# Tighter one-hot windows, table blocks in one go, flushes at their own group's end, and an even pace in a graph kernel

## The chip, the cores and the metric

The kernel runs on one core of one Trainium2 chip. The metric is the device time of one execution in microseconds, as the median of several runs; lower is better. The core has TensorE (PE; its weight loads are listed as PEld), VectorE (DVE), ScalarE (ACT), GpSimd (POOL) and SyncE (SP), which each work through their own instructions in order.

## The reference

12500 nodes have a row x of 128 numbers. 200000 edges have a source node, a destination node and one of four types; the edges come sorted by destination, and the destinations are drawn as 12500 u^2, so low nodes have many edges and high nodes few. What is computed:

```
h   = relu(layernorm(x))                       # 12500 x 128
out = x
for each edge e:  out[dst[e]] += h[src[e]] @ W[type[e]] + b[type[e]]
```

W is 4 x 128 x 128, b is 4 x 128, all in f32.

## The kernel before

**Chunks and the two parts.** The sorted edges are cut into 1563 chunks of 128. The first 480 chunks, those of the nodes with many edges, are the *dense part*: for a node the kernel counts how often each (source, type) occurs, in `count` (line 802: one-hots L814, L818, L819 on VectorE, matmul L823 into pt, ScalarE copies the counts out, L826), and multiplies the counts with the whole table of h in `multiply` (line 847: loads hs from htab, matmuls pa L858, then py L873 and an add to `acc`). The dense part goes over 14 batches of up to 92 nodes; the first has no batch before it whose products could run beside its counts.

**The other 1083 chunks** are taken in 70 groups: 66 of 16 chunks (groups 0 to 65, FULL is 66) and small ones of 12, 8, 4 and 3. `gather` (line 443) fetches a chunk's 128 source rows with one indirect DMA on GpSimd's queue (L449), eight to a buffer `hm`, a half group; there are five such buffers. `sum_up` (line 461) does a group:

1. A one-hot for each chunk on VectorE (L471): its columns are type times window plus the node's offset from the chunk's first node. The *window* is the number of nodes that a chunk can span, a number fixed when the kernel is built (`window_of`, line 111), so a one-hot has K = 4 x window columns.
2. TensorE counts the types per node (L494; L492 in the raw groups), ScalarE copies that (cnt, L498).
3. In four steps of four chunks, TensorE sums the rows by type and node (ps, L509; three bf16 matmuls a chunk, of K columns), and ScalarE copies the sums (sb, L516).
4. TensorE multiplies with b (L524) and, in four f32 matmuls of 16 x window columns, with W (py, L526; the trace has two records of each).
5. VectorE adds each chunk's window of py to `ring` (L538), 16 adds at places that are read from memory. The ring holds 2048 nodes.

**The raw groups.** Groups 0 to 7 (RAW is 8) gather rows of x, and normalise them themselves in f32 (`stats` L382, `normalize` L401, one-hots `ohf`, ps in f32), because the table `htab` of normalised rows isn't there yet. It is made meanwhile: `table` (line 413) is a generator of three steps for a block of rows, two blocks a group: the first normalises on ScalarE and copies a bf16 part (L419), the second subtracts it on VectorE (L421) and copies the next part (L422), the third subtracts again (L424) and sends the block with a DMA on SyncE's queue (L425). Step one runs at the group's start (L1008), steps two and three behind the group's own two halves (`table_steps`, L484). `make_slots` prepares the dense part's slots in the same stage.

**The flushes.** Nodes that no later chunk can touch leave the ring, four blocks of 128 nodes at a time: `put_out` (line 577) and `leave` (line 560) transpose them on TensorE (L568), add x on VectorE (xo, L571), send them by DMA (L573) and clear the ring (memset, L586). `goes` (line 615) says behind which group each flush is due; the first, at group 8, adds 1280 nodes of the ring to `acc` instead. A flush that is due behind a group is put on a list (L1069), and made in the next group, behind its sums and ahead of its py (L521).

**The order.** From group 8 on the dense part is a generator (`dense_work`, line 903) whose steps are issued between the groups' steps: `pace` (line 890) says from the columns of both kinds of work how far the dense part should be after each step. In the first batch a count slot weighs 3.5 times as much as later (`alone_slot`, L907). A scheduler then orders each engine's instructions.

Of the kernel before, what the change touches and what calls it, by code (L numbers as in the profile page):

```python
# [35 lines left out]
F32 = mybir.dt.float32  # L36
BF16 = mybir.dt.bfloat16
# [32 lines left out]
def kernel(  # L70
# [37 lines left out]
    starts_of = [sum(levels[:k]) for k in range(len(levels) + 1)]  # L108
    NS = starts_of[-1]

    def window_of(c):

        c = C0 + (c - C0) // G * G
        a_node = E * ((((c + G) * P / E) ** 2 + 1 / N) ** 0.5 - (c + G) * P / E)
        return next((n for n in range(12, WIN, 4) if (n - 1) * a_node > P + 6 * P**0.5), WIN)

    NDT = -(-ND // P)

# [288 lines left out]
        load_nodes(xt, j0, j1)  # L407
        seen_x[j0] = xt, stats(lambda k: xt[:r, k, :], j1 - j0, r, aheads, "t")


    tabling = []

    def table(j0, j1, r):
        n = j1 - j0
        xt, of = seen_x.pop(j0)
        h = npool.tile([P, XG, D], F32, name="h")
        h3 = npool.tile([P, XG, 3, D], BF16, name="h3")
        normalize(lambda k: xt[:r, k, :], lambda k: h[:r, k, :], n, r, of)
        nc.scalar.copy(h3[:r, :n, 0, :], h[:r, :n, :])  # L419
        yield True  # L420
        nc.vector.tensor_sub(h[:r, :n, :], h[:r, :n, :], h3[:r, :n, 0, :])  # L421
        nc.scalar.copy(h3[:r, :n, 1, :], h[:r, :n, :])  # L422
        yield True
        nc.vector.tensor_sub(h3[:r, :n, 2, :], h[:r, :n, :], h3[:r, :n, 1, :])  # L424
        nc.sync.dma_start(  # L425
            htab.rearrange("(p j) f -> p j f", j=NW)[:, j0:j1, :], h3[:, :n].rearrange("p j c d -> p j (c d)")
        )

    def table_steps():
        for t in list(tabling):  # L430
            if next(t, None) is None:
                tabling.remove(t)

    tables = []
    for j0, j1 in ((0, NL), (NL, NW)):
# [20 lines left out]
        return lambda i, c, n: got[i // HG][:, (i % HG * n + c) * D : (i % HG * n + c + 1) * D]  # L456

    waiting = []
    flushing = []

    def sum_up(t0, g, rows, raw, last):
        win = window_of(C0 + t0)
        K = NT * win
        if raw:
            oh = npool.tile([P, G, P], F32, name="ohf")[:, :, :K]
        else:
            while waiting:
                waiting.pop()()
            oh = opool.tile([P, G, P], BF16, name="oh")[:, :, :K]
        for i in range(g):  # L470
            nc.vector.tensor_scalar(  # L471
                oh[:, i, :], (iota_f if raw else iota_b)[:, :K], keyf[:, t0 + i : t0 + i + 1], None, ALU.is_equal
            )
        if raw:
            for h0 in range(0, g, HG):
                row = lambda k: rows(h0 + k, 0, 1)
                n = min(HG, g - h0)
                of = stats(row, n, P, npool, "")
                normalize(row, row, n, P, of)

                with tc.issue_after(of[2]):
                    while waiting and h0 + HG >= g:
                        waiting.pop()()
                    table_steps()  # L484
        sb = spool.tile([P, G * P], F32, name="sb")[:, : G * K].rearrange("p (g t n) -> p g t n", g=G, t=NT)
        def types():

            ohv = oh.rearrange("p g (t n) -> p g t n", t=NT)
            pc = s_ps.tile([R, G * WIN], F32, name="ps")[:, : G * win].rearrange("p (g n) -> p g n", g=G)
            for t in range(NT):  # L490
                if raw:
                    nc.tensor.matmul(pc[:, :g, :], pick_f[:, t, :], ohv[:, :g, t, :], start=(t == 0), stop=(t == NT - 1))  # L492
                else:
                    nc.tensor.matmul(  # L494
                        pc[t * CG : (t + 1) * CG, :g, :], three, ohv[:, :g, t, :], start=True, stop=True, tile_position=(0, t * CG)
                    )
            cnt = spool.tile([R, G * WIN], BF16, name="cnt")[:, : G * win].rearrange("p (g n) -> p g n", g=G)
            nc.scalar.copy(cnt[:, :g], pc[:, :g])  # L498
            return cnt

        R = N3 if raw else P
        cnt = None if raw else types()
        nparts = 1 if raw else 3
        for i0 in range(0, g, SG):
            i1 = min(i0 + SG, g)
            ps = s_ps.tile([P, SG, P], F32, name="ps")[:, :, :K]
            for i in range(i0, i1):
                for c in range(nparts):
                    mm = nc.tensor.matmul(  # L509
                        ps[:, i - i0, :],  # L510
                        rows(i, c, nparts),
                        oh[:, i, :],
                        start=(c == 0),
                        stop=(c == nparts - 1),
                    )
            nc.scalar.copy(sb[:, i0:i1].rearrange("p g t n -> p g (t n)"), ps[:, : i1 - i0, :])  # L516
            yield i1 / g, mm.ins
        if raw:
            cnt = types()

        while flushing:  # L521
            put_out(*flushing.pop(0))
        py = (x_ps.tile([P, G * WIN], F32, name="pt") if last else y_ps.tile([P, G * WIN], F32, name="py"))[:, : G * win].rearrange("p (g n) -> p g n", g=G)
        nc.tensor.matmul(py[:, :g, :], b12 if raw else b128, cnt[:, :g, :], start=True, stop=False)  # L524
        for t in range(NT):
            mm = nc.tensor.matmul(py[:, :g, :], wsb[:, t, :], sb[:, :g, t, :], start=False, stop=(t == NT - 1))  # L526

        def add_up():
            _, at = nc.values_load_multi_w_load_instructions(
                brow[0:1, t0 : t0 + g],  # L530
                engines=[DVE],
                min_val=0,
                max_val=RING - 1,
                skip_runtime_bounds_check_because="the row is clamped to this range on the chip",
            )
            for i in range(g):
                to = ring[:, bass.ds(at[i], win)]
                nc.vector.tensor_tensor(to, to, py[:, i, :], ALU.add)  # L538

        if raw or t0 + g == TM:  # L540
            waiting.append(add_up)
        else:
            add_up()
        yield 1, mm.ins
# [59 lines left out]

    flushes = [(ja, jb, due(jb)) for ja, jb, _ in flushes]


    ends_in = [12, 8, 4, 3]
    FULL = (TM - sum(ends_in)) // G
    r = TM - sum(ends_in) - FULL * G  # L610
    sizes = [G] * FULL + ([r] if r else []) + ends_in
    starts = [sum(sizes[:i]) for i in range(len(sizes))]
# [289 lines left out]

    def dense_work():


        a_slot = float(NB)
        alone_slot = 3.5 * NB  # L907
        a_node = NW * 3.0 * NT
        total = dense_columns() + sum(len(slots_of(u)) for u in units(batches[0])) * (alone_slot - a_slot)
        gone = 0.0  # L910
        before = None
        for vs in batches + [None]:
            steps = {}
            now = None
            if vs:
                now = vs, dense.tile([P, NW, VB // 2 * NT], U16, name="counts")
                steps[count(*now)] = sum(len(slots_of(u)) for u in units(vs)) * (a_slot if before else alone_slot)
            if before:
                steps[multiply(*before)] = len(before[0]) * a_node
            done = {st: 0.0 for st in steps}  # L920
            while done:
                st = min(done, key=done.get)
                part = next(st, None)
                if part is None:
                    del done[st]
                    gone += steps[st]
                else:
                    done[st] = part
                    yield (gone + sum(done[st] * steps[st] for st in done)) / total
            before = now  # L930
# [19 lines left out]
    for gi, (t0, g) in enumerate(zip(starts, sizes)):  # L950
        raw = gi < RAW
        if gi == 0:
# [44 lines left out]
            for t in range(NT):  # L997
                for c in range(3):
                    k = c * NT + t
                    nc.sync.dma_start(b128[t * CG + c : t * CG + c + 1, :], b12[k : k + 1, :])  # L1000
            tabling += [table(*a) for a in tables[:2]]
            table_steps()
            for a in tables[2:4]:
                look(*a)
            done = 2
        elif raw:
            rows = gather(t0, g, x, D)
            tabling += [table(*a) for a in tables[done : done + 2]]  # L1008
            table_steps()
            for a in tables[done + 2 : done + 4]:  # L1010
                look(*a)
            done += 2
            if gi == 1:
                prep_dense()
            elif gi == 3:
                prep_edges(1, 3, prep, QB)
        else:
            rows = gather(t0, g, htab, D3)

            q = (t0 + 8 * G) // P  # L1020
            if (t0 + 8 * G) % P < G and 3 <= q < BM:
                prep_edges(q, q + 1, later, 1)
        if gi == RAW - 1:
            assert done >= len(tables) and not tabling

        behind = ExitStack()
        if gi >= FULL:
# [38 lines left out]
                leave(ja, jb, acc, ja * P)  # L1066
        for (ja, jb, _), i in zip(flushes, goes):
            if i == gi < final - 1:
                flushing.append((ja, jb, True))  # L1069
        if gi == final:  # L1070

            for ahead in (True, False):
# [137 lines left out]
```

## Time and profile before

| | before |
|---|---|
| median of 3 runs | 1923.1 us (1918.42 to 1924.55) |
| profiled execution | 1924.55 us |
| its span, from the first to the last instruction | 1922.7 us |
| mean granted TensorE clock | 0.878 of full speed |
| instructions | 30094 |
| gathers from htab / from x | 955 / 128 |
| last ring add of group 7, of group 9, of the last group | 318.4, 373.8, 1915.8 us |

The profile is of one execution. The busy time of an engine is given in us and as a share of the span. The chain that ended last is followed back from the last instruction, at each step to what released it. A line such as `ACT sb L516 <- remote: 259.0, 51, 8.9` says that ScalarE, at line 516, waited 259.0 us in all, 51 times, at most 8.9 us; "remote" or "unknown queue" is a releaser that the profile doesn't name. A line of the chain or the timeline begins with its start and its length in us; x12 is twelve instructions in a row. By stage the run falls into the raw groups (0 to some 300 us), the main stage with the dense part beside the groups (to some 1870 us), and the end.

### The profile page before, as it was taken

How to read it: one execution, taken by the hardware profiler on the slowest of the kernel's cores; microseconds unless marked ns; L12 is line 12 of the kernel's file. 1: busy time of each engine (PE TensorE's matmuls, PEld its weight loads, DVE VectorE, ACT ScalarE, POOL GpSimd, SP SyncE). 2: the span in 40 equal slices, each digit the busy share in tenths (PEclk: the TensorE clock that was granted, in tenths of full speed). 3: DMA queues.
4: the chain of work that ended last, by engine and by line, in shares of the span. 5: the costliest groups of instructions: out<-in, count | busy, mean ns of one | idle time of the engine just before them, and what ended most of it. 6: DMA issues, size and time to landing. Idle time of an engine off the chain costs nothing.

```text
span 1922.7 us, 30094 instructions
## 1 busy us (share of the span) xinstructions
PE 1421.5 (74%) x9606; PEld 879.8 (46%) x9606; DVE 968.3 (50%) x5293; ACT 589.9 (31%) x1920; POOL 1048.6 (55%) x1093
## 2 busy tenths in 40 slices
PE   0354665776778778787787888787878888788885
PEld 0232432554445445454454455454545545454553
DVE  3666753755556554354344444454565555555233
ACT  3464633222132232323232322323232332323111
POOL 7463455353555546555455566455565666565561
PEclk9995665787888889899799889888999999998998
DMA  4342223454555445455455555455555555455552
GB/s 137 91 138 77 99 82 97 121 153 115 145 148 144 135 124 167 134 175 161 130 154 157 163 150 174 132 169 155 153 151 169 166 146 175 144 162 139 163 166 72
DMA packets 137427, 270.75 MB, mean 141 GB/s; under 512 B 26316, under 2 KB 73598, under 8 KB 137262
## 3 DMA queue, kind: packets, MB, share of 16 engines
q1 hardware_dynamic: 87326, 166.44, 28.2%
q0 software_dynamic: 49936, 102.34, 19.8%
q8 instruction: 76, 1.25, 0.3%
q14 instruction: 89, 0.73, 0.1%
HBM read 252.64 MB, written 16.03 MB: 140 GB/s over the span
## 4 chain that ended last, share of the span: by engine, by line
PE 55%; another core or an unknown queue 14%; DVE 12%; issue 11%; ACT 5%; POOL 2%; DMA 1%; SPq 0%; DVEq 0%; ACTq 0%; POOLq 0%
PE pa L858 29%; PE pt L823 10%; PE ps L509 6%; PE py L526 6%; ACT counts L826 3%; DVE o L819 2%; POOL hm L449 2%; DVE st L382 1%; DVE ring L538 1%; DVE o L818 1%; DVE oh L471 1%; ACT sb L516 1%; PE py L873 1%; PE ps L492 1%
## 5 line engine op out<-in xcount | busy, mean ns | idle before, releaser
L449 POOL DMA_INDIRECT hm<-htab,srcT x955 | 921.5, 965 | 732.8 <-issue 253.0
L858 PE MATMUL pa<-counts,hs 128*128 128x368 fp8e4 (+1 forms) x4116 | 786.1, 339 | 34.1 <-issue 31.9
L858 PEld LDWEIGHTS <-hs 128*128 128x128 bf16 x4116 | 425.9, 104 | 376.4 <-issue 180.2
L823 PE MATMUL pt<-o,o 128*128 128x392 bf16 x1083 | 307.0, 358 | 178.6 <-ACT counts L826 64.7
L826 ACT ACTIVATE counts<-pt 128x392 uint16<-128x392 f32 x630 | 310.3, 504 | 346.3 <-PE pt L823 146.5
L819 DVE TENSOR_SCALAR o<-iota_n,hkT 128x392 bf16<-128x392 f16 x1083 | 350.6, 324 | 0.6 <-issue 0.4
L516 ACT COPY sb<-ps 128x256 f32<-128x256 f32 (+5 forms) x271 | 111.4, 417 | 538.7 <-remote 259.0
L538 DVE TENSOR_TENSOR ring<-ring,py 128x16 f32 (+4 forms) x1056 | 178.8, 169 | 149.5 <-remote 39.8
L814 DVE TENSOR_SCALAR o<-iota_b,loT 128x128 bf16<-128x128 bf16 x375 | 96.2, 257 | 286.5 <-remote 133.8
L509 PE MATMUL ps<-oh,hm 128*128 128x64 bf16 (+4 forms) x2865 | 174.1, 206 | 72.3 <-issue 67.2
L509 PEld LDWEIGHTS <-hm 128*128 128x128 bf16 x2865 | 143.4, 102 | 135.0 <-issue 107.5
L471 DVE TENSOR_SCALAR oh<-iota_b,keyT 128x64 bf16<-128x64 bf16 (+4 forms) x955 | 166.7, 255 | 65.4 <-remote 22.4
L818 DVE TENSOR_SCALAR o<-iota_b,loT,byT 128x128 bf16<-128x128 bf16 x333 | 108.0, 324 | 176.0 <-remote 73.5
L823 PEld LDWEIGHTS <-o 128*128 128x128 bf16 x1083 | 102.8, 104 | 190.9 <-issue 86.2
L449 POOL DMA_INDIRECT hm<-in_x_dram,srcT x128 | 125.6, 981 | 106.1 <-PE ps L509 67.3
L526 PE MATMUL py<-sb,wsb 128*128 128x384 f32 (+4 forms) x528 | 165.9, 460 | 0.7 <-issue 0.7
L509 PE MATMUL ps<-ohf,hm 128*128 128x48 f32 x256 | 60.1, 397 | 107.8 <-ACT hm L401 107.8
L826 ACT ACTIVATION_READ_ACCUMULATOR counts<-pt 128x1 f32 x630 | 131.9, 209 | 0.0
L526 PEld LDWEIGHTS py<-sb,wsb 128*128 128x128 f32 x528 | 107.3, 214 | 51.8 <-issue 26.4
L498 ACT CAST cnt<-ps 128x256 bf16<-128x256 f32 (+7 forms) x70 | 28.5, 407 | 292.6 <-PE ps L494 80.5
L509 PEld LDWEIGHTS ps<-ohf,hm 128*128 128x128 f32 x256 | 54.1, 305 | 126.2 <-ACT hm L401 112.7
L818 DVE TENSOR_SCALAR o<-iota_b,loT 128x128 bf16<-128x128 bf16 x375 | 97.0, 259 | 16.5 <-PE pt L823 12.7
(188 smaller groups left out, 647.2 us busy)
## 6 DMA issues: line engine op xcount, KB each, us to landing
hs<-htab SPq DMA_DIRECT2D x336, 384.0 KB
hm<-htab,srcT POOLq DMA_INDIRECT x955
htab<-h SPq DMA_DIRECT2D x11, 768.0 KB
xo<-in_x_dram SPq DMA_DIRECT2D x23, 256.0 KB
out_dram<-xo SPq DMA_DIRECT2D x23, 256.0 KB
xt<-in_x_dram SPq DMA_DIRECT2D x6, 512.0 KB
hs<-htab SPq DMA_DIRECT2D x14, 192.0 KB
xt<-in_x_dram SPq DMA_DIRECT2D x5, 448.0 KB
```

Of the source, the lines that this page charges most:

```text
L449: nc.gpsimd.indirect_dma_start(out=rows[:, (i - h0) * width : (i - h0 + 1) * width], out_offset=None, in_=table, in_offset=bass.IndirectOf ...
L471: nc.vector.tensor_scalar(oh[:, i, :], (iota_f if raw else iota_b)[:, :K], keyf[:, t0 + i : t0 + i + 1], None, ALU.is_equal)
L509: mm = nc.tensor.matmul(ps[:, i - i0, :], rows(i, c, nparts), oh[:, i, :], start=(c == 0), stop=(c == nparts - 1),)
L516: nc.scalar.copy(sb[:, i0:i1].rearrange("p g t n -> p g (t n)"), ps[:, : i1 - i0, :])
L526: mm = nc.tensor.matmul(py[:, :g, :], wsb[:, t, :], sb[:, :g, t, :], start=False, stop=(t == NT - 1))
L538: nc.vector.tensor_tensor(to, to, py[:, i, :], ALU.add)
L814: nc.vector.tensor_scalar(o1[:, k, :], iota_b, loT[:, s : s + 1], None, ALU.is_equal)
L818: nc.vector.tensor_scalar(o1[:, k, :], iota_b, loT[:, s : s + 1], by, ALU.is_equal, ALU.mult)
L819: nc.vector.tensor_scalar(o2[:, k, :], iota_n, hkT[:, s : s + 1], None, ALU.is_equal)
L823: nc.tensor.matmul(pb, o1[:, k, :], o2[:, k, :], start=first, stop=last)
L826: nc.scalar.activation(counts[:, :, i * NT : (i + 1) * NT], pb.rearrange("p (b t) -> p b t", t=NT), AF.Copy, accum_out=both[:, i : i + 1],)
L858: nc.tensor.matmul(pa[:, : nv * NT], hs[:, j - j0, c * D : (c + 1) * D], counts[:, j, : nv * NT], start=(j == 0 and c == 0), stop=(j == NW ...
```

## The change

Four things are changed. (1) `window_of` goes in steps of 2 from 8 with five deviations of room, where it went in steps of 4 from 12 with six; the small last groups share one number; the buffers of the one-hots and of sb are as wide as the widest window needs. (2) `table` is no longer a generator: a block is made in one go at the start of its raw group. (3) A flush is made at the end of the group behind which it is due, not in the next group. (4) The first dense batch's count slots weigh as much as those of the others.

```diff
     def window_of(c):
-        c = C0 + (c - C0) // G * G
-        a_node = E * ((((c + G) * P / E) ** 2 + 1 / N) ** 0.5 - (c + G) * P / E)
-        return next((n for n in range(12, WIN, 4) if (n - 1) * a_node > P + 6 * P**0.5), WIN)
+        m = min((c - C0) // G, FULL)
+        end = (C0 + (m + 1) * G if m < FULL else T) * P / E
+        a_node = E * ((end**2 + 1 / N) ** 0.5 - end)
+        return next((n for n in range(8, WIN, 2) if (n - 1) * a_node > P + 5 * P**0.5), WIN)
...
     def table(j0, j1, r):
...
         nc.scalar.copy(h3[:r, :n, 0, :], h[:r, :n, :])
-        yield True
         nc.vector.tensor_sub(h[:r, :n, :], h[:r, :n, :], h3[:r, :n, 0, :])
         nc.scalar.copy(h3[:r, :n, 1, :], h[:r, :n, :])
-        yield True
         nc.vector.tensor_sub(h3[:r, :n, 2, :], h[:r, :n, :], h3[:r, :n, 1, :])
...
-            oh = opool.tile([P, G, P], BF16, name="oh")[:, :, :K]
+            oh = opool.tile([P, G, KM], BF16, name="oh")[:, :, :K]
...
-                with tc.issue_after(of[2]):
-                    while waiting and h0 + HG >= g:
-                        waiting.pop()()
-                    table_steps()
+            with tc.issue_after(of[2]):
+                while waiting:
+                    waiting.pop()()
...
-        while flushing:
-            put_out(*flushing.pop(0))
...
-        alone_slot = 3.5 * NB
...
-        total = dense_columns() + sum(len(slots_of(u)) for u in units(batches[0])) * (alone_slot - a_slot)
+        total = dense_columns()
...
-                steps[count(*now)] = sum(len(slots_of(u)) for u in units(vs)) * (a_slot if before else alone_slot)
+                steps[count(*now)] = sum(len(slots_of(u)) for u in units(vs)) * a_slot
...
-            tabling += [table(*a) for a in tables[done : done + 2]]
-            table_steps()
+            for a in tables[done : done + 2]:
+                table(*a)
...
             if i == gi < final - 1:
-                flushing.append((ja, jb, True))
+                put_out(ja, jb, True)
```

The windows, in nodes, by group:

| groups | before | after |
|---|---|---|
| 0 to 7 | 12 | 10 |
| 8 to 12 | 12 | 12 |
| 13 to 15 | 16 | 12 |
| 16 to 24 | 16 | 14 |
| 25 to 28 | 16 | 16 |
| 29 to 32 | 20 | 16 |
| 33 to 40 | 20 | 18 |
| 41 to 44 | 20 | 20 |
| 45 to 49 | 24 | 20 |
| 50 to 57 | 24 | 22 |
| 58 to 60 | 24 | 24 |
| 61 to 65 | 28 | 24 |
| 66 to 69 (the small ones) | 28 | 26 |

More of the change, by code (lines that the diff above doesn't have):

```diff
@@ L109 @@
     NS = starts_of[-1]
+    ends_in = [12, 8, 4, 3]
+    FULL = (TM - sum(ends_in)) // G
     def window_of(c):
-        c = C0 + (c - C0) // G * G
-        a_node = E * ((((c + G) * P / E) ** 2 + 1 / N) ** 0.5 - (c + G) * P / E)
-        return next((n for n in range(12, WIN, 4) if (n - 1) * a_node > P + 6 * P**0.5), WIN)
+        m = min((c - C0) // G, FULL)
+        end = (C0 + (m + 1) * G if m < FULL else T) * P / E
+        a_node = E * ((end**2 + 1 / N) ** 0.5 - end)
+        return next((n for n in range(8, WIN, 2) if (n - 1) * a_node > P + 5 * P**0.5), WIN)
     NDT = -(-ND // P)
@@ L408, in look @@
         seen_x[j0] = xt, stats(lambda k: xt[:r, k, :], j1 - j0, r, aheads, "t")
-    tabling = []
     def table(j0, j1, r):
@@ L427, in table @@
         )
[L429 to L432, printed above, removed]
     tables = []
@@ L458 @@
     waiting = []
-    flushing = []
+    KR, KM = NT * window_of(C0 + RAW * G - 1), NT * window_of(T - 1)
     def sum_up(t0, g, rows, raw, last):
@@ L464, in sum_up @@
         if raw:
-            oh = npool.tile([P, G, P], F32, name="ohf")[:, :, :K]
+            oh = npool.tile([P, G, KR], F32, name="ohf")[:, :, :K]
         else:
@@ L479, in sum_up @@
                 normalize(row, row, n, P, of)
-                with tc.issue_after(of[2]):
-                    while waiting and h0 + HG >= g:
-                        waiting.pop()()
-                    table_steps()
-        sb = spool.tile([P, G * P], F32, name="sb")[:, : G * K].rearrange("p (g t n) -> p g t n", g=G, t=NT)
+            with tc.issue_after(of[2]):
+                while waiting:
+                    waiting.pop()()
+        sb = spool.tile([P, G * KM], F32, name="sb")[:, : G * K].rearrange("p (g t n) -> p g t n", g=G, t=NT)
         def types():
@@ L605 @@
     flushes = [(ja, jb, due(jb)) for ja, jb, _ in flushes]
-    ends_in = [12, 8, 4, 3]
-    FULL = (TM - sum(ends_in)) // G
     r = TM - sum(ends_in) - FULL * G
@@ L1000 @@
                     nc.sync.dma_start(b128[t * CG + c : t * CG + c + 1, :], b12[k : k + 1, :])
-            tabling += [table(*a) for a in tables[:2]]
-            table_steps()
+            for a in tables[:2]:
+                table(*a)
             for a in tables[2:4]:
@@ L1007 @@
             rows = gather(t0, g, x, D)
-            tabling += [table(*a) for a in tables[done : done + 2]]
-            table_steps()
+            for a in tables[done : done + 2]:
+                table(*a)
             for a in tables[done + 2 : done + 4]:
@@ L1023 @@
         if gi == RAW - 1:
-            assert done >= len(tables) and not tabling
+            assert done >= len(tables)
         behind = ExitStack()
```

## The prediction, made blind

> **What bounds the kernel now.** I read the page's busy times first, then the chain that ended last, then the waits, then the chain and the timeline of one stretch in the middle of the run.
>
> ```profile
> PE 1421.5 (74%) x9606; PEld 879.8 (46%) x9606; DVE 968.3 (50%) x5293; ACT 589.9 (31%) x1920; POOL 1048.6 (55%) x1093
> ...
> PE 55%; another core or an unknown queue 14%; DVE 12%; issue 11%; ACT 5%; POOL 2%; DMA 1%; SPq 0%; DVEq 0%; ACTq 0%; POOLq 0%
> PE pa L858 29%; PE pt L823 10%; PE ps L509 6%; PE py L526 6%; ACT counts L826 3%; DVE o L819 2%; POOL hm L449 2%; DVE st L382 1%; DVE ring L538 1%; DVE o L818 1%; DVE oh L471 1%; ACT sb L516 1%; PE py L873 1%; PE ps L492 1%
> ```
>
> The reader is to see that TensorE is the fullest engine and carries most of the chain, half of that in the dense part (L858, L823), which the change leaves alone. What it makes smaller, ps L509 and py L526, is 6% each. The waits tell who waits for TensorE:
>
> ```profile
> POOL hm L449 <- issue: 289.0, 946, 0.6
> ACT sb L516 <- remote: 259.0, 51, 8.9
> POOL hm L449 <- PE pt L823: 246.2, 54, 19.3
> POOL hm L449 <- PE ps L509: 230.7, 44, 15.2
> ```
>
> GpSimd's gathers stand 477 us (246.2 + 230.7) in 98 waits until TensorE frees a row buffer, so from group 8 on the gathers follow TensorE. But the second line (columns: us in all, times, longest) is a wait of another kind: ScalarE and VectorE stand together for up to 9 us with no releaser that the profile names. In the trace about 116 such joint stalls, one per half group, end within some 0.1 us of the landing of the eighth gather of a batch; the batches start 13.7 us apart on average, and some 60% of them 13 us or less, where eight gathers of 1.25 us with a landing of about 2 us leave little to shorten. TensorE starves in these stalls:
>
> ```profile
> 1010.25 0.18 DVE L538 TENSOR_TENSOR ring<-ring,py 128x20 f32 x1
> 1010.49 0.17 DVE L538 TENSOR_TENSOR ring<-ring,py 128x20 f32 x1
> ...
> 1018.64 0.31 DVE L818 TENSOR_SCALAR o<-iota_b,loT,byT 128x128 bf16<-128x128 bf16 x1 [7.05 <-remote]
> 1018.87 0.17 DVE L538 TENSOR_TENSOR ring<-ring,py 128x20 f32 x1
> ...
> 1019.59 1.44 PE L823 MATMUL pt<-o,o 128*128 128x392 bf16 x3 [6.00 <-ACT counts L826]
> ```
>
> A stall of 7 us cuts a group's 16 ring adds in two; TensorE goes on at 1019.59, and the last add starts only at 1021.56.
>
> **Part 1, the windows.** Groups 0 to 7 go from 12 nodes to 10; of the 62 others 16 keep their window, 29 lose 2 and 17 lose 4, as both rules give them. From group 8 on the sum of window times chunk falls from 19316 to 17374 columns, by 1942. Prices come from the chain's pieces, which hold several instructions of one line back to back:
>
> ```profile
> 589.38 1.73 PE py L526 x8
> 594.32 0.35 PE ps L509 x12
> ```
>
> ```profile
> 1721.66 2.58 PE py L526 x8
> 1734.16 0.51 PE ps L509 x12
> ```
>
> The first pair is a group with window 16 (64 columns of L509, 256 of L526), the second one with 24 (96 and 384). py: 2.58 - 1.73 = 0.85 us for 128 columns, 6.6 ns a column for its eight records; times 1942 is **12.9 us**. ps: 42.5 ns against 29 ns each, 0.42 ns a column; a piece with window 12 shows 12 in 0.30 us, 25 ns each, so below 64 columns only 0.25 ns a column is saved. Over the 62 later groups that is **8.8 us**. L494 and L524 lose 1942 columns each, at 0.42 ns **1.6 us**. Together 23.3 us of TensorE. ScalarE's sb copies (313 ns at 192 columns, 534 at 448, 0.86 ns a column) lose 7768 columns, 6.7 us; VectorE's ring adds 2.7 us (160 ns at window 16, 182 at 28). Those two engines are 31% and 50% busy, so I cost their share at nothing; if they were on the chain, 9.4 us more would go.
>
> How much of 23.3 us reaches the end? Lower end: only the batches that start more than 13 us apart, 43 of 116, can be shortened, 37%, so 9 us. Upper end: all of it and the copies and adds, 33 us. In the chain from 1000 to 1060 us TensorE's lines make 74%, the rest is unknown queues (11%), issue (9%) and ScalarE. I take 74%, **17 us**, as the row nearest to the stretch concerned. What is late next where TensorE is shortened is the gather batch.
>
> On the first 300 us I put no gain: the eight f32 groups lose 8 columns a chunk, but TensorE is busy 135.6 of 300 us there and waits for normalised rows (ps L509 for ACT hm L401, 107.8 us).
>
> **Part 2, tables at once.** Instructions stay the same in number; they move. In the order of ScalarE's instructions group 0's own normalisation now stands behind 12 more table normalisations (0.384 us from start to start) and 3 more copies (1.03 us), 7.7 us; in later raw groups one table's worth stands ahead, but an equal lot has gone from between the halves. The htab DMAs go out up to a half group earlier, behind which the first table gather stood (17.7 us, once). The raw stage can shift by the whole 7.7 us or win a few: -5 to +8, and I take **+2**, because ScalarE is busy 138.5 of the 300 us and can catch up before group 7.
>
> **Part 3, flushes at their own group's end.** Before, the four transposes (L568) stand directly ahead of the next group's py, in most flushes with 14 to 18 us of TensorE work behind their own group's py. After, in the order of TensorE's instructions, fourteen of the twenty with transposes have some 4 to 6 us of work between (12 to 24 sums and 15 to 22 pa for the late nine), six have 12 to 16. The transposes need all 16 ring adds. At 0.24 us from start to start those take 3.9 us and would just be done; but cut by a stall they take 3.2 to 13.8 us, 6.9 in the median. The wait is added on TensorE, and behind it queue the next sums, pa and counts, for which ScalarE and GpSimd wait. On VectorE, xo (0.69 us) and the memset (0.48) now follow the adds at once, ahead of the next one-hots: 1.2 us that was there before, at another place. Lower end 0: the wait falls wholly into a gap in which TensorE starves anyway. Upper end 2 us a flush, from the stretch above (1021.56 against 1019.59), 40 us over twenty. In before, L568 waited for ring adds 5.7 us in 5 cases. I take 0.4 us a flush, **+8**, nearer to those 5.7 us.
>
> ```profile
> 1007.49 0.44 PE pt L568 x4
> 1008.06 2.15 PE py L526 x8
> 1010.68 0.54 PE ps L509 x12
> ...
> 1022.87 0.80 PE ps L509 x12
> ```
>
> Twelve sums take 0.43 us at window 20 at full speed; 0.80 us after the stall, where the granted clock from 1020 to 1024 reads 0.50. [...]
>
> **Part 4, the pace of the first dense batch.** Without the weight of 3.5, group 8 takes on 53 instead of 16 count slots and 60 pa: 37 x 0.166 + 60 x 0.156 = 15.5 us of TensorE work come earlier, and the later groups have as much less. From 300 to 420 us TensorE is busy 64%, so there is room, but the counts there are drained by ScalarE at 0.71 us each. -8 (half of it fills idle time) to +8 (the drains set the pace); I take **0**.
>
> **Sum.** -17 + 2 + 8 + 0 = -7 us. Against the profiled execution's 1924.55 us (span 1922.7) this gives 1917.5; the median of the runs, 1923.1, is 1.5 us lower, so the forecast is **1916 us**.
>
> **Rivals.** (a) *All of the window's saving shows and the flush waits cost nothing*: -23.3 + 2 = -21, so **1902**. For: GpSimd waits 477 us for TensorE. Against: the joint stalls. (b) *The gather batches hide it*: with 60% of the batches at their floor and the rest bound by something else, -9 + 8 + 2 = +1, so **1924**; then TensorE's time falls and the span doesn't. (c) *Slower, by the early transposes*: TensorE, in order, stands at the first transpose until a ring add that a stall delayed. With 2 us a flush it is -17 + 40 + 2 = +25, so **1948**; with 1.2 us, +9, **1932**. It decides for slower from 0.75 us a flush (15 / 20). For: the median 6.9 us of the adds against 4 us of work ahead. Against: the idle gap is there anyway.
>
> **Chances.** A measurement of this kernel can tell about 0.3% (5.8 us) from no change, so faster means below 1917.3 and slower above 1928.9. The forecast (1910 to 1922) has 0.38, of which 0.22 lies in faster; (a) 0.20, faster; (b) 0.14, of which 0.10 within the bound and 0.04 above; (c) 0.28, slower. Faster 0.42, same 0.26, slower 0.32. The range from 1899 to 1937 takes in (a), (b) and the nearer half of (c).
>
> **What would show it.** py x8 pieces of 1.3 to 2.8 us by the new window and PE's busy time down by 23 to 26 us would show part 1; gather batches that start 13.4 instead of 13.7 us apart its passage. The transposes' idle time on ring adds, 5.7 us before, tells part 3: near 14 us would be the forecast, 25 or more rival (c). The first ps L509 and group 7's last ring add (318.4 us before) show part 2, group 8's and 9's adds (339, 374 us) part 4. I am wrong if the stalls themselves grow or shrink, which I cannot price, since their cause isn't shown.

## The result, and the profile after

The changed kernel takes 1976.15 us (median of 4 runs, 1967.27 to 1978.85) against 1922.49 us before: ratio 1.0274, 95% interval 1.0237 to 1.031. It is 54 us slower, where 1916 us was forecast with a range up to 1937. The profiled execution takes 1976.76 us, its span is 1975.0 us, and the granted clock is 0.852 (before 0.878).

The page after, busy times and chain:

```profile
PE 1411.9 (71%) x9606; PEld 874.4 (44%) x9606; DVE 971.4 (49%) x5301; ACT 587.8 (30%) x1920; POOL 1045.3 (53%) x1093
...
PE 53%; another core or an unknown queue 14%; DVE 12%; issue 11%; ACT 4%; POOL 1%; DMA 0%; DVEq 0%; ACTq 0%; POOLq 0%
PE pa L846 28%; PE pt L811 10%; PE ps L503 6%; PE py L517 6%; DVE ring L529 2%; ACT counts L814 2%; DVE oh L466 2%; DVE o L807 2%; DVE st L387 1%; DVE o L806 1%; POOL hm L444 1%; PE pt L559 1%; DVE ohf L466 1%; PE py L861 1%
```

No engine works noticeably more than before (VectorE 3 us more); TensorE works 9.6 us less (1421.5 before), and every share falls because the span grows. So 52 us of waiting came, and the shares of the chain don't say where. The waits do:

```profile
POOL hm L444 <- PE ps L503: 263.0, 48, 21.5
ACT sb L510 <- remote: 250.2, 53, 10.1
POOL hm L444 <- PE pt L811: 236.0, 36, 35.8
...
POOL hm L444 <- ACT sb L510: 38.7, 5, 26.6
```

Read the third column, the longest wait, and not the sums: GpSimd's gathers, which never waited longer than 19.3 us before, now stand 35.8, 26.6 and 21.5 us at a time. The last ring add of each group places the loss: group 19 ends 10 us earlier than before, group 20 9.5 us later, group 24 25 us later, group 27 41 us later, the last one 52. The jumps come in the groups after flushes (19, 23, 26, 30, ...): 43 us are lost by group 31, 38 are left at group 47, and the last 14 come behind it.

What such a jump looks like on GpSimd and on ScalarE, after the flush of group 23 (timeline; idle time before an instruction and its releaser in brackets):

```profile
831.85 0.95 POOL L444 DMA_INDIRECT hm<-htab,srcT  x1 [0.30 <-issue]
833.10 0.95 POOL L444 DMA_INDIRECT hm<-htab,srcT  x1 [0.30 <-issue]
869.84 0.94 POOL L444 DMA_INDIRECT hm<-htab,srcT  x1 [35.78 <-PE pt L811]
```

```profile
814.86 0.37 ACT L510 COPY sb<-ps 128x256 f32<-128x256 f32 x1 [0.24 <-PE pt L286]
834.80 0.37 ACT L492 CAST cnt<-ps 128x256 bf16<-128x256 f32 x1 [8.61 <-remote]
864.58 0.37 ACT L510 COPY sb<-ps 128x256 f32<-128x256 f32 x1 [3.63 <-PE ps L503]
```

For 49.7 us, from 814.86 to 864.58, no sums are copied out, and no row buffer comes free; GpSimd fills what it has and stands from 834 to 870. From 400 us on, the longest pause between two sb copies was 25.1 us before. Pauses over 20 us in the same part after: 45.7 (at 691 us), 49.7 (815), 28.6 (1047), 25.0 (1499).

The order of TensorE's instructions shows why. Its work is priced with the trace's median start-to-start times (pa 0.156 us, pt 0.166, a py record of window 16 0.216), so the lengths are estimates of undisturbed work. A *stretch* is the work between two sums; a *pause*, as above, is the time that passed.

```
                                 before  after
own py to transposes, median      15.5    3.6  us of TensorE work
counts (pt) in between, median     16      0
longest stretches without sums    14.1   30.8, 29.7, 24.5, 22.4  us
py behind sums of the next group, before: groups 20, 24, 56, 64 (5 to 36 sums)
                                  after:  groups 20, 24, 27, 28, 31, 64 (26 to 72 sums), six more (2 to 12)
```

With the flush at its own group's end, the transposes' tile is taken from the three buffers pt before the next group's counts ask for one. In the order hardly a count stands ahead of the transposes any more; sums of the next group are drawn ahead, and the counts, pa and py follow in one piece of up to 31 us. The piece of 30.8 us is the one in the pause of 49.7 us. That pause also holds a wait without a named releaser (8.61 us, the second ScalarE line above) and other gaps. Behind group 47 the order has no stretch longer than 14 us, so the last 14 us of the loss have another cause.

### The profile page after: what moved, and what is told of

Its sections match the earlier page's. It is cut to its first block, busy times and chain, and to the rows that moved or that the text cites. A ratio compares the mean times of both kernels' runs of the same rounds, so it can differ in the third digit from the quotient of the medians.

```text
span 1975.0 us, 30109 instructions
## 1 busy us (share of the span) xinstructions
PE 1411.9 (71%) x9606; PEld 874.4 (44%) x9606; DVE 971.4 (49%) x5301; ACT 587.8 (30%) x1920; POOL 1045.3 (53%) x1093
## 3 DMA queue, kind: packets, MB, share of 16 engines
q1 hardware_dynamic: 87326, 166.44, 27.7%
## 4 chain that ended last, share of the span: by engine, by line
PE 53%; another core or an unknown queue 14%; DVE 12%; issue 11%; ACT 4%; POOL 1%; DMA 0%; DVEq 0%; ACTq 0%; POOLq 0%
PE pa L846 28%; PE pt L811 10%; PE ps L503 6%; PE py L517 6%; DVE ring L529 2%; ACT counts L814 2%; DVE oh L466 2%; DVE o L807 2%; DVE st L387 1%; DVE o L806 1%; POOL hm L444 1%; PE pt L559 1%; DVE ohf L466 1%; PE py L861 1%
## 5 line engine op out<-in xcount | busy, mean ns | idle before, releaser
L846 PEld LDWEIGHTS <-hs 128*128 128x128 bf16 x4116 | 418.6, 103 | 395.6 <-issue 202.8
L811 PE MATMUL pt<-o,o 128*128 128x392 bf16 x1083 | 318.4, 368 | 160.0 <-ACT counts L814 65.9
L529 DVE TENSOR_TENSOR ring<-ring,py 128x20 f32 (+7 forms) x1056 | 177.4, 168 | 188.6 <-PE py L517 48.6
L510 ACT COPY sb<-ps 128x160 f32<-128x160 f32 (+9 forms) x271 | 104.1, 389 | 535.2 <-remote 250.2
L466 DVE TENSOR_SCALAR oh<-iota_b,keyT 128x56 bf16<-128x56 bf16 (+7 forms) x955 | 172.4, 253 | 173.5 <-remote 105.0
L503 PE MATMUL ps<-oh,hm 128*128 128x56 bf16 (+7 forms) x2865 | 163.3, 204 | 109.0 <-issue 82.6
L503 PEld LDWEIGHTS <-hm 128*128 128x128 bf16 x2865 | 137.8, 103 | 179.2 <-issue 155.3
L811 PEld LDWEIGHTS <-o 128*128 128x128 bf16 x1083 | 107.8, 106 | 188.0 <-issue 101.4
L517 PE MATMUL py<-sb,wsb 128*128 128x160 f32 (+7 forms) x528 | 155.6, 438 | 2.5 <-issue 1.2
L503 PE MATMUL ps<-ohf,hm 128*128 128x40 f32 x256 | 60.1, 398 | 94.0 <-ACT hm L406 72.2
L492 ACT CAST cnt<-ps 128x224 bf16<-128x224 f32 (+9 forms) x70 | 26.7, 381 | 281.0 <-remote 84.3
```

What stands on the lines that cost most here:

```text
L466: nc.vector.tensor_scalar(oh[:, i, :], (iota_f if raw else iota_b)[:, :K], keyf[:, t0 + i : t0 + i + 1], None, ALU.is_equal)
L503: mm = nc.tensor.matmul(ps[:, i - i0, :], rows(i, c, nparts), oh[:, i, :], start=(c == 0), stop=(c == nparts - 1),)
L811: nc.tensor.matmul(pb, o1[:, k, :], o2[:, k, :], start=first, stop=last)
L846: nc.tensor.matmul(pa[:, : nv * NT], hs[:, j - j0, c * D : (c + 1) * D], counts[:, j, : nv * NT], start=(j == 0 and c == 0), stop=(j == NW ...
```

## The experiments

Theory A, that the early flushes are the loss, against B (the new windows upset the order) and C (only the two together) came first. Then theory L (the stretches without sums stop the gathers) stood against W (the transposes wait for ring adds) and T (the work on VectorE).

The experiments fell in six sets, each with the kernel before on the same chip, and **the sets are of two kinds**. In the first result, e1 to e8 and e18 the kernel before takes 1922 to 1962 us; in e9 to e17 it takes 1419 to 1422 us, the same program. The last section tells what the traces show of it. Ratios are compared within a kind; I call them the sets *with* and *without unnamed waits*. The expectations speak of two kinds of chips, but that isn't shown: the record gives the chip the number 0 both for e5 to e8 (1924 us) and for e9 to e12 (1422 us).

**e1, part 3 alone.**

```diff
-                flushing.append((ja, jb, True))
+                put_out(ja, jb, True)
```

> The kernel before with only part 3: every flush is made at its own group's end. Theory A (the early flushes are the loss: the transposes stand on TensorE ahead of the dense work and wait for ring adds, and what queues behind them starves): 40 to 75 us slower than before, 1962 to 1998 us, with the loss in the groups right behind the flushes. Theory B (the loss comes with the new windows, which change the order of all work; the early flush costs what the prediction took for it): 0 to 15 us slower, 1922 to 1937 us. Theory C (the early flush hurts only with the narrow windows, as a combination): within 5 us of before.

Measured 2010.95 us against 1956.12: 1.0265 (1.0211 to 1.0319). This one line is enough for a loss as large as the whole one: A is right on where it comes from. In its order there is one stretch of some 30 us, and eleven py stand behind 2 to 50 sums of the next group; its longest pause between sums is 49.8 us, at 1299 us. The wait that A names is small in its trace:

```profile
PE pt L568 <- DVE ring L538: 8.0, 7, 1.8
```

**e2, the change without part 3.** The opposite edit in the changed kernel, with `flushing` back ahead of py.

> The changed kernel with only part 3 undone: flushes again in the next group, behind its sums. Theory A: the whole loss goes and the saving of the windows shows: 1902 to 1918 us. Theory B: it stays slower than before by 35 to 55 us, 1957 to 1977 us. Theory C: like A, 1902 to 1918 us.

Measured 1942.93 against 1956.12: 0.9945 (0.9908 to 0.9982), 11 us faster (4 to 18). The loss is gone; the longest stretch is 14.7 us. One pause of 31.0 us (at 684 us) stands in its trace all the same, so not every long pause comes from a stretch in the order.

**e3 and e4, part 1 and part 4 alone**, `window_of` with its widths, and `alone_slot = a_slot`.

> The kernel before with only part 1, the windows with their buffer widths. Theory A and theory C: 8 to 21 us faster than before, 1901 to 1914 us. Theory B: 30 to 55 us slower than before, 1952 to 1977 us.

> The kernel before with only part 4: the first batch's count slots weigh 1 instead of 3.5. Theory A: within 8 us of before, with groups 8 to 11 some 12 us later and that won back by group 19, as the traces of before and after show it. Rival D (the dense work that is brought forward upsets the main stage for good): 15 us slower or more.

e3: 1934.52, 0.9895 (0.9837 to 0.9952), 21 us faster (9 to 32): B and C fall. e4: 1927.51, 0.9828 (0.9771 to 0.9886), a gain that nobody had expected; its size is uncertain, as the kernel before spread from 1941 to 1966 us in this set.

**e5, the changed kernel with another buffer for the transposes.**

```diff
-        pt = x_ps.tile([P, OT, DO], F32, name="pt")
+        pt = (s_ps.tile([P, OT, DO], F32, name="ps") if of is ring else x_ps.tile([P, OT, DO], F32, name="pt"))
```

> The changed kernel whole, early flushes included, with one difference: the flush's transposes write into a buffer of the sums' pool (ps, three buffers) and not into one of the three buffers pt through which the counts go. In the order of TensorE's instructions the long stretches of dense work without any sums (four of 22 to 30 us in the changed kernel) are then gone, the longest is 16 us; the transposes still stand right behind the ring adds. Theory L (the loss comes from these stretches, in which no row buffer is freed and the gathers stop): the loss goes, 8 to 25 us faster than before, ratio 0.987 to 0.996. Theory W (the transposes' own wait for ring adds on TensorE is the loss): 30 to 55 us slower than before, ratio 1.015 to 1.03.

Measured 1987.74 against 1924.29: 1.0326 (1.0294 to 1.0357). Theory L alone is wrong here, and the profile shows that L and W both have a part. The long pauses are gone (27.7 us is the longest from 400 us on): groups 20 to 38 end within 9 us of before, where the changed kernel was up to 43 us late. But in this order the transposes stand straight behind their own py with no work between, and now the waits name them:

```profile
PEld ps L559 <- DVE ring L529: 103.7, 19, 8.4
...
PE ps L559 <- DVE ring L529: 101.4, 22, 8.2
```

TensorE stands 101.4 us in 22 waits, 4.6 us a wait, until the ring adds are done; from group 39 on the groups fall behind by some 6 us a flush, 64 us in the end. In the changed kernel the same row of the waits says 10.9 us in 7:

```profile
PE pt L559 <- DVE ring L529: 10.9, 7, 4.3
```

So in these two kernels the early flush is paid either as a wait on TensorE or, where other work is put ahead of the transposes, in the order of that other work.

**e6 and e18, stretches without any early flush**, the dense work held back in the kernel before.

```diff
         n = gi - RAW
+        for h in (22, 27, 32, 37, 42):
+            if gi == h or gi == h + 1 and part < 0.5:
+                n, part = h - RAW, 0.0
```

> The kernel before, flushes untouched, but the dense work is held back for one and a half groups at groups 22, 27, 32, 37 and 42 and then caught up, so that TensorE's order has five stretches of 21 to 25 us without sums. Theory L: 20 to 50 us slower than before, ratio 1.01 to 1.026, with holes of more than 20 us between sums and GpSimd's gathers standing in them. Theory W: within 8 us of before, since the same work is done and no flush moves.

> The kernel of e6, five forced stretches of 21 to 25 us without sums, once more. On a chip without the unnamed waits, where before takes about 1420 us: if a stretch costs by stopping the gathers only where it is drawn out by those waits (in e6 the sums paused for up to 46 us), ratio 1.0 to 1.01, since GpSimd has some 40 us of work ahead. If a stretch costs by its length alone: 1.015 or more. On a chip with the waits: 1.038 to 1.045 as in e6.

e6: 2001.3 against 1924.29, 1.0419 (1.0389 to 1.045); e18, again with unnamed waits, 2027.54 against 1962.07, 1.0316 (1.0262 to 1.0371). Five stretches of 21 to 25 us cost 62 to 81 us with no flush moved, so L's mechanism is shown to work by itself, and by more than the 1.01 to 1.026 that L had expected (e18 stays under its 1.038 to 1.045); what W and T name isn't there. The longest pauses of e6 are 46.1 and 43.7 us. In e6's waits the gathers stand as in the changed kernel:

```profile
POOL hm L449 <- PE ps L509: 272.5, 47, 27.1
POOL hm L449 <- PE pt L823: 263.9, 39, 31.3
```

**e7 and e8, part 2 alone, and parts 1 and 4.** e7 takes the `yield`s out of `table`; e8 is e3 with e4's line.

> The kernel before with only part 2, the table blocks in one go. TensorE's order from group 8 on is the same as before. Prediction's step: +2 us, between -5 and +8. Theory F (it brings a few us back at group 7 after delays of up to 11 us on the way, as the traces of before and after show): 0 to 5 us faster.

> The kernel before with parts 1 and 4, flushes deferred and tables in steps. If the gains of the two add (1.05% and 1.7% faster when alone): 2 to 3% faster than before, ratio 0.970 to 0.980. If pace alone was mostly a better order by chance, which the windows change anyway: 0.5 to 1.5% faster, ratio 0.985 to 0.995.

e7: 1927.37 against 1924.29, 1.001 (0.998 to 1.004). e8: 1918.49, 0.9975 (0.9952 to 0.9998): the two gains don't add.

**e9, e14 and e17, the changed kernel with the transposes in py's buffer**, `y_ps.tile(..., name="py")` in place of e5's `s_ps` tile.

> The changed kernel whole, early flushes included, but the transposes write into the one buffer of py, which the ring adds have just freed. In TensorE's order the transposes then stand 3.5 to 10 us of work behind their own py with counts in between, and no stretch without sums is longer than 16 us. Theory L+W (an early flush costs either way: as a wait of some 5 us on TensorE where it stands straight behind its py, or as long stretches without sums where it shares the counts' buffers): with both mostly avoided the loss goes, ratio to before 0.985 to 1.005. Rival T (an early flush costs by its work on VectorE, which comes ahead of the next one-hots and counts, wherever the transposes write): ratio 1.02 to 1.03 as in the changed kernel.

> As e9, the changed kernel with the transposes in py's buffer, now with the changed kernel on the same chip. On a chip with the unnamed waits, theory L+W: ratio 0.985 to 1.005, 20 to 60 us faster than the changed kernel; rival T: within 8 us of the changed kernel. On a chip without them: ratio 0.995 to 1.0.

> The kernel of e9 and e14 once more, in the hope of a chip with the unnamed waits, where before takes 1920 to 1960 us. There, theory L+W: ratio 0.985 to 1.005; rival T: 1.02 to 1.03. If before takes about 1420 us again: 0.997 to 0.999, and the question stays open.

0.9975 (0.9966 to 0.9985), 0.9982 (0.9973 to 0.9992) and 0.9972 (0.9959 to 0.9985), at 1416 to 1418 us. All three fell in sets without unnamed waits. There it is the fastest version tried, and faster than the changed kernel (e13); on the other kind it wasn't measured.

**e10, the flush after the first of the next group's four steps; e11 and e12, e3 and e4 again.**

> The kernel before, with the flush made in the next group after its first of four steps of sums, instead of after all four. TensorE's order has 5.0 us of work (median) between the own py and the transposes where before has 15.5 and the early flush alone 3.7, and one stretch of 28 us without sums. Theory L+W: between before and the early flush alone, ratio 1.005 to 1.02. Rival T: as before, within 0.5%, since the one-hots of the next group are made first.

> The kernel before with part 1 alone once more, on another chip: 23.3 us less TensorE work by the prediction's prices. If the saving of 1.05% that the first run showed is the windows' own: ratio 0.985 to 0.994. If it was that chip's: 0.995 to 1.0.

> The kernel before with part 4 alone once more. The prediction put it at 0, between -8 and +8 us. If the 1.7% of the first run is the pace's own: ratio 0.977 to 0.989. If not, 0.995 to 1.003.

e10: 1.0009 (0.9999 to 1.0019). e11: 0.9989 (0.998 to 0.9998). e12: 1.0001 (0.9992 to 1.001). Without unnamed waits none of this matters much: there the gathers run almost without a break, from 4.1 to 1403.7 us of e12's 1418, and are the bound, so less work for TensorE (23.3 us by the prediction) shows as 1.6 us.

**e13, e15 and e16, the change, part 3 alone and e5 without unnamed waits.**

> The changed kernel itself, unaltered, beside the kernel before on the same chip. If the chip shows the waits with no named releaser and before takes about 1925 us: ratio 1.02 to 1.035, as in the first comparison. If it shows none and before takes about 1421 us (the gathers then run without a break): the stretches without sums are shorter than the gathers' lead, so ratio 1.0 to 1.01.

> As e1, part 3 alone. On a chip with the unnamed waits: ratio 1.02 to 1.032 as in e1. On a chip without them: theory L+W says 1.0 to 1.01, since the ring adds are no longer cut in two and the gathers' lead covers the stretches.

> As e5, the changed kernel with the transposes in a sums buffer, straight behind their own py with no work between. On a chip with the unnamed waits: ratio 1.028 to 1.036. On a chip without them: the 16 ring adds still take about 4 us, so the wait on TensorE stays at 3 to 4 us a flush, 60 to 80 us on TensorE, but the gathers are the bound there: ratio 1.0 to 1.03.

e13: 1422.29 against 1419.46, 1.0021 (1.0011 to 1.0031). e15: 1.0024 (1.0014 to 1.0033). e16: 1455.1, 1.0249 (1.0232 to 1.0267). The stretches are in e13's program as in the first result's, and its trace has pauses between sums of 36.9 us (at 563 us), 32.8, 28.9 and 22.4; yet GpSimd hardly notices:

```profile
POOL hm L444 <- issue: 307.1, 1008, 0.3
ACT sb L510 <- PE ps L503: 291.1, 144, 10.7
...
POOL hm L444 <- PE pt L811: 19.7, 24, 8.9
```

The gathers' waits for TensorE come to 19.7 us here, the longest to 8.9, where the first result has 236.0 and 35.8 in the same row. The gathers are some 16 us ahead of the sums that use them (median of e13, last gather of a step to its sb copy), so the five buffers are far from full, and a pause mostly fills them. Beside e12, whose order has no long stretch, the groups of e13 fall 25 us behind by group 33 and have won that back by group 52. In the first result the gathers were some 60 us ahead, the buffers full, and a pause stopped them at once. e16's wait, on the other hand, costs on both kinds: 80.9 us on TensorE in 23 waits.

## Why the prediction was wrong

**The step that failed is part 3**, "I take 0.4 us a flush, +8", with its upper end of 40 us. By e1 it is 52 us (41 to 62), some 2.6 us a flush over the twenty with transposes; in the changed kernel, against e2, some 65 (54 slower and 11 faster, from two sets). The rival that named it, (c), had the side right, and the mechanism half right: as a wait of TensorE at the first transpose it is 101 us where nothing is put ahead (e5), but in the changed kernel that wait is only 10.9 us, and most of the loss, the 43 us by group 31, comes with stretches without sums that stop the gathers: it stays away in e5, whose order has none of them. The prediction took the order of TensorE's instructions only for the distance between py and transposes, and read it as cover. It called it 4 to 6 us; by the prices above it is 3.5 to 5.6, hardly more than the 3.9 us of the ring adds. And it didn't ask what had been moved to make that cover. The same order has the four stretches of 22 to 31 us and the py behind up to 72 sums; the test given at the end, "near 14 us would be the forecast, 25 or more rival (c)", looked at the wrong row, which reads 19.2 us (waits of TensorE and its weight loads together) and decides nothing.

The prediction's last sentence named another way to be wrong, that the unnamed waits grow. They did, from 834 us in 192 waits to 983 in 207 over the engines, but this alone doesn't explain the loss: e3, which is faster, has 1021 us in 229 and e5, which is slower, 717 in 188.

**Part 1 agrees in the sets with unnamed waits.** Forecast 17 of 23.3 us; e3 measures 21 (9 to 32). A py piece of window 22 takes 2.37 us, where the same group (56) took 2.58 with window 24, as priced.

```profile
1734.30 2.37 PE py L517 x8
```

But TensorE's busy time in the changed kernel fell by 9.6 us only, not by 23 to 26, and no other pair of traces shows the whole sum: e3 (another set) has 16.8 us less than before, e11 13.9 less than e12 beside it (clocks 0.942 and 0.946). In the changed kernel the granted clock reads 0.84 against 0.88 from 420 to 1000 us. In the traces of before and after a pa of 368 columns starts 0.156 us (median) after the pa ahead of it where the clock reads 1.00, and 0.307 us where it reads 0.50, so part of the saved work may have come back as slower work; no run here separates this term, nor shows what lowers the clock.

**Part 2** was forecast at +2; e7 gives +2 us (-4 to +8), and the trace of the changed kernel shows the shift inside the raw stage: group 3 ends 11.2 us later, group 7 4.1 us earlier. **Part 4** was forecast at 0; the shift is there (groups 8 to 11 end 11 to 13 us later, won back by group 13), and e12 gives 0.01%. That e4 gained 1.7% stays open: from 400 us on its trace has no pause over 20 us between sums, where before has two (22.1 and 25.1), but e8 shows that the gain doesn't survive another order.

**The rivals**: (a), -21, is reached by the windows alone (e3, -21), but not by the change without the early flush (e2, -11, 4 to 18 us faster); (b) is what the windows do where the gathers are the bound (e11). The sum of the four parts alone, -21 + 2 + 52 - 33 to 0, spans 0 to 33 us; the change measured 54. The rest is the combination; what fits it is that with the new windows and pace the early flush gets four long stretches instead of one.

**What stays open**: what the unnamed waits are; where the last 14 us of the loss come from; whether py's buffer makes the early flush free where they occur, which was measured only where they don't; how e1's 52 us divide between its one stretch (25 us are lost in group 40 alone), the other displaced py and the flush's own work on VectorE, which now stands ahead of the next one-hots (theory T: 1.2 us a flush by the prediction's lengths, 24 in all, and no run with unnamed waits separates it); and why the scheduler draws the sums ahead, which I only inferred from the buffer that was shared, as e5 and e9 show that the order follows it.

## What to carry to other kernels

When a step is moved in a kernel whose order a scheduler makes, compare the whole order of the busiest engine before and after, not only the place of the step: list the longest stretches in which the work that frees the scarce buffer doesn't occur. Ask which rotating buffer the moved step takes, and who would have had it; an accumulator that the step's own predecessor has just freed was a better place here than a buffer of the stream that must go on (0.2 to 0.3% faster than before against 2.5% slower, both without unnamed waits). And a pause cost where the producer already stood at full buffers (the gathers some 60 us ahead, 2.7% slower); where it was itself the bound, its empty buffers absorbed most of the pause (some 16 us ahead, 0.2% slower).

## What the runs showed of the hardware

The kernel before takes 1922 to 1962 us in some of the sets and 1419 to 1422 us in others. The changed kernel itself was traced in both kinds, in the first result and as e13, with gathers of nearly the same length (961 and 972 ns). e13 shows:

```profile
PE 1253.1 (88%) x9606; PEld 827.2 (58%) x9606; DVE 972.2 (68%) x5301; ACT 588.6 (41%) x1920; POOL 1060.0 (75%) x1093
```

Its waits have no row with a releaser "remote"; the first result has 983 us of them in 207 waits over the engines. There, ScalarE starts an sb copy 2.2 us (median from group 8 on; in a tenth of the cases over 6.7 us) after the last matmul of its sums has ended by the trace, and in e13 0.04 us. So in the sets with unnamed waits ScalarE often goes on late, after a matmul whose end the trace shows well before. Whether the news of the end is late, or the matmul itself, whose end is modelled in the trace, isn't shown. With it the granted clock is lower (0.852 against 0.943), and TensorE is 1411.9 us busy instead of 1253.1 with the same instructions. What makes the difference isn't shown by any run either, and it is larger than every effect of this change.
